# Two-layer vision tower, layer-1 attention: first pair's transposed features fetched in layer 0's feed-forward into an older tile; normed pairs in six buffers and made first in their step

## The chip, the cores and the metric

The kernel runs on one core of one Trainium2 chip. The metric is the device time of one execution in microseconds (us), as the median of three executions. All arithmetic is in fp32.

## The reference, cut to what matters

32 images of 256x256 pixels are cut into 256 patches each; a patch becomes a token of 256 features. Two layers follow, each with an attention part and a feed-forward part, and each part adds its result to `h`. The change lies where layer 0's feed-forward ends and layer 1's attention begins, so only these two are shown (biases, all of which the kernel keeps, are left out here).

```
# layer 0, feed-forward on x = layernorm(h): 127 tokens of each image are selected by a weight
y = gelu(sel @ w1) @ w2 * w_sel          # sel: the selected rows of x
h = h + (x with y added at the selected rows)

# layer 1, attention on x = layernorm(h)
key   = tanh(gelu(x @ Wk1) @ Wk2) * freq * pi
query = tanh(gelu(x @ Wq1) @ Wq2) * freq * pi
V     = x @ Wv
retrieved[l] = sum over m <= l of V[m] * sum_k cos(key[m,k] - query[l,k])
retrieved    = retrieved / sqrt(position * 64)
h = h + x + layernorm(retrieved) @ Wo
```

After it comes layer 1's feed-forward, a per-head attention with four expert queries, which takes the last third of the time.

## The kernel before

Everything is one function, `vit_tower`. `h` stays in SBUF for all 32 images (`H[b]`, 128 partitions x 2 halves x 256 features). The order of instructions on each engine is written out by hand (`tc.manual_schedule`, for all that follows here): each engine runs its instructions in program order, and a tile's buffers (`bufs=n`) make a new writer wait for the last readers of the buffer that it takes over.

**Layer 0's feed-forward** works on quads of four images. Its loop runs t from 0 to 31 (`END_C` is 32, line 907), and `step_c(t)` (line 901) issues by the table `ORDER_C` what of each quad is due: `hidden_c` (w1 and GELU), `made` (w2; each image's result `cy` is written to DRAM as `results` by SyncE, line 871), `fetch` (the results gathered back by rank with indirect DMAs on GpSimd, line 879), `update` (the result added into `H` and the row statistics taken, lines 890, 124, 125). The table reaches past the loop: the last quad's `fetch` and `update` come at 32, 33 and 34, which are issued within layer 1's attention (at its t = 6, 9 and 12).

**Layer 1's attention** works on 16 pairs of two images. What it needs per pair, with the lines that the prediction speaks of:

- `norm_d` (825): the normed tokens `x = h * rstd + (1 - mean * rstd)`, on VectorE. For each image two small operations on `d_one` (832, 833) and two on 128x256 (835). Pairs 0 and 1 are made inside layer 0's loop, at its t = 30, into buffers of `cx`; all later pairs into buffers of `dx`, of which there are four, so two pairs.
- `blocks_d` (841): VectorE turns the pair in blocks of 32x32 (197) into `dxB` (pairs 0 and 1: into `cs`), and SyncE writes it to the DRAM tile `c_turned` (200), which has two buffers.
- `moved_d` (934), by `moved` (202): SyncE reads `c_turned` back, rearranged to feature-major order, into `dxT` (203), which has two buffers. The two DMAs together with the blocks make the transpose.
- `hidden` (937): TensorE multiplies `dxT` with `wk1` (i = 0) and `wq1` (i = 1), eight matmuls each, and ScalarE applies GELU into `dg0`/`dg1` (946).
- `phases` (948): TensorE takes `dg` through `wk2`, `wq2`; ScalarE tanh into `dturn` (963); VectorE wraps the phase in `dz` (965 to 969); ScalarE takes the sine (970).
- `match` (972): TensorE multiplies the sines; VectorE masks into `dat` (985).
- `memory` (988): TensorE multiplies the normed tokens (`cx` or `dx`) with `dat`; ScalarE copies to `dm` (998). These are the last reads of the pair's normed tokens on TensorE.
- `output` (1001): TensorE multiplies `dm` with `wvo`; VectorE takes statistics (1009, 1010); GpSimd makes `d_rs` (149, 150).
- `add_output` (1016): VectorE adds the scaled result to `H` (1019), which also frees the four PSUM banks of `output`. `stats_e` (1021): the row statistics for the next part, with `rs_e` on GpSimd.
- `residual_d` (846): GpSimd adds the normed tokens and a constant row to `H`, four operations per pair (849, 850).

The loop of this stage (line 1030) runs over t, three steps to a pair; `do(step, which)` issues `which` for the pair u with t = 3u + step. For t above 5 the order is: steps with t = 1 mod 3: `add_output` of the pair two back, `match` of the pair before, `stats_e` two back, `residual_d`; steps with t = 2 mod 3: `hidden` of pair u, `memory` of pair u - 1, and then `norm_d`, `blocks_d`, `moved_d` of pair u + 1; steps with t = 0 mod 3: `phases` of u and `output` of u - 1. The first steps are special: at t = 1 `moved_d` of pair 0; at t = 2 `hidden` of pair 0 and `moved_d` of pair 1; at t = 5 `hidden` of pair 1 with `match` of pair 0 between its halves, `residual_d` of pair 1, and then the norm of pair 2.

Layer 0's pools are closed ahead of this loop (lines 925, 926), and the pools `d_2` and `d_8` take over their memory: `dxT`, `dg`, `dz` in `d_2`; `dat`, `dm`, `dx`, `dxB` in `d_8`. The pool `c_x`, with the eight `cx` buffers and the one tile `blocks` (4 KB per partition; its last use is the turning of layer 0's last quad), stays open to the end of the attention (line 1074).

Of the kernel before, what the change touches and what calls it, by code (L numbers as in the profile page):

```python
# [33 lines left out]
F32 = mybir.dt.float32  # L34
# [6 lines left out]
P = 128  # L41
B, N, D = 32, 256, 256
NC = N // P
# [37 lines left out]
def vit_tower(tc, a, out):  # L81
# [15 lines left out]
    def bank():  # L97
        return ppool.tile([P, 512], F32, name="bank", tag="bank")

    def col(name, i=0):  # L100
        c = COLS[name][0] + i
        return cols[:, c : c + 1]
# [12 lines left out]
    def mm(o, lhsT, rhs, first=True, last=True):  # L115
        nc.tensor.matmul(o, lhsT, rhs, start=first, stop=last)  # L116
# [4 lines left out]
    def stats(st, i, c, x):  # L121

        six = spool.tile([P, 6], F32, name="six")
        nc.vector.bn_stats(six, x)  # L124
        nc.vector.bn_aggr(st[:, i, c, :], six)
# [26 lines left out]
    def pow_rstd_of(pair, b, images):  # L152
        st, rs, i = at(pair, b)
        q = slice(i * NC, (i + images) * NC)
        pow_rstd(rs[:, q], st.rearrange("p i c s -> p (i c) s")[:, q, 1])

    def new_stats(name):
        return [
            (
                cpool.tile([P, HALF, NC, 2], F32, name=f"st_{name}{k}", tag=f"st{k}", bufs=2),  # L160
                cpool.tile([P, HALF * NC], F32, name=f"rs_{name}{k}", tag=f"rs{k}", bufs=2),
            )
            for k in range(2)
        ]

    def at(pair, b):

        st, rs = pair[b // HALF]
        return st, rs, b % HALF
# [22 lines left out]
    def blocks_turned(y, xs, d):  # L192

        y5 = y.rearrange("p (f s t) -> p s f t", f=4, t=32)
        n = 8 // len(xs)
        for j, x in enumerate(xs):
            nc.vector.transpose(
                y5[:, j * n : (j + 1) * n], x.rearrange("p c (k f t) -> p (c k) f t", k=2, f=4)
            )
        nc.sync.dma_start(d.rearrange("i q x -> (i q) x"), y)  # L200

    def moved(xT, d):
        nc.sync.dma_start(xT, d.rearrange("i q (f x) -> (q f) i x", f=4))
        return xT.rearrange("p i (s k t) -> p k s i t", k=2, t=32)
# [12 lines left out]
    px = passing_x.enter_context(tc.tile_pool(name="c_x", bufs=1, reuse_waits="tile"))  # L217
# [86 lines left out]
    with (  # L304
# [7 lines left out]
        for k, n in enumerate(PARTS):  # L312
            f = sum(PARTS[:k])
            x, w = pw.tile([P, n, N], F32, name=f"patch0_{k}"), pw.tile([P, n, D], F32, name=f"tokW{k}")
# [4 lines left out]
        p = bank()  # L319
# [116 lines left out]
    with (  # L436
# [80 lines left out]
        def ranks(b0, p):  # L517
            for j in range(2):
                rank_c(b0 + j, *normed_c[b0][j], p[:, j * N : (j + 1) * N])

        def norms_c(b0):
            normed_c[b0] = [norm_c(b0 + j) for j in range(2)]

        def residuals_c(b0):
            for j in range(2):
                residual_c(b0 + j, normed_c[b0][j][0])
# [126 lines left out]
    for i in range(2):  # L653
        s, t = slice(i * HD, (i + 1) * HD), slice((1 - i) * HD, (2 - i) * HD)
# [186 lines left out]
    def blocks_d(b0, s, pool, name, shape, bufs):  # L841
        y = pool.tile(shape, F32, name=name, bufs=bufs)
        s.d = pdram.tile([4, 32, 4 * N], F32, name="c_turned", bufs=2)
        blocks_turned(y.rearrange("p j d -> p (j d)"), s.xs, s.d)
# [7 lines left out]
    with region_c:  # L852
        st_d = new_stats("d")

        def hidden_c(b0, s, half):
            if half == 0:
                s.hT = p2.tile([P, 8, 4 * P], F32, name="hT")
            for m in range(4 * half, 4 * half + 4):
                p = bank()
                for k in range(2):  # L860
                    mm(p, w1[:, k, m * P : (m + 1) * P], s.f[:, k], k == 0, k == 1)
                nc.scalar.activation(s.hT[:, m, :], p, AF.Gelu_apprx_tanh, bias=col("b1", m))  # L862

        def made(b0, s, half):
            for j in range(2 * half, 2 * half + 2):
                p = bank()
                for m in range(8):
                    mm(p[:, 0:D], s.hT[:, m, j * P : (j + 1) * P], w2[:, m, :], m == 0, m == 7)
                y = p2.tile([P, D], F32, name="cy", bufs=4)
                nc.vector.tensor_tensor(y, p[:, 0:D], row_c("b2"), ALU.add)  # L870
                nc.sync.dma_start(results[b0 + j][:], y)

        def fetch(b0, s, half):
            s.y = s.y if half else []
            for b in range(b0 + 2 * half, b0 + 2 * half + 2):
                y = px.tile([P, NC, D], F32, name="cx", bufs=8)
                for c in range(NC):
                    k = b * NC + c
                    nc.gpsimd.indirect_dma_start(
                        y[:, c, :], None, results[b][:], bass.IndirectOffsetOnAxis(rank_of[:, k : k + 1], 0)  # L880
                    )
                s.y.append(y)

        def update(b0, s, half):
            for j in range(2 * half, 2 * half + 2):
                b = b0 + j
                st, rs, i = at(st_d, b)
                for c in range(NC):
                    k = b * NC + c
                    nc.vector.scalar_tensor_tensor(  # L890
                        H[b][:, c, :], s.y[j][:, c, :], w_kept[:, k : k + 1], H[b][:, c, :], ALU.mult, ALU.add
                    )
                    stats(st, i, c, H[b][:, c, :])
            pow_rstd_of(st_d, b0 + 2 * half, 2)

        ORDER_C = ((0, hidden_c, 0), (1, hidden_c, 1), (2, made, 0), (-3, blocks_c, 0), (-2, moved_c, 0), (-8, first_ranks, 0),
                   (3, made, 1), (4, fetch, 0), (5, fetch, 1), (5, update, 0), (6, update, 1))

        def step_c(t):
            for at_step, do, j in ORDER_C:
                u, r = divmod(t - at_step, 4)
                if r == 0 and 0 <= u < B // 4 and (u > 1 or do is not first_ranks):
                    do(4 * u, quads[u], j)

        END_C = 4 * (B // 4 - 1) + 4
        pairs = [Pair() for _ in range(B // 2)]
        preparing = prepare()
        for t in range(END_C):  # L910
            if t == 0:
                norms_c(B - 2)
                residuals_c(B - 2)
            if t == END_C - 2:
                for u in range(2):
                    norm_d(2 * u, pairs[u], px, "cx", 8)
                for u in range(2):
                    blocks_d(2 * u, pairs[u], p0, "cs", [P, 4, D], 2)
            step_c(t)
            if t < 2:  # L920
                ranks(B - 4 + 2 * t, turn_weights(B - 4 + 2 * t))
            if t >= 8:
                next(preparing, None)
        passing.close()
# [5 lines left out]
    with (  # L930
# [99 lines left out]
        for t in range(3 * (NP - 1) + 8):  # L1030
            def do(step, which, *more):
                u, r = divmod(t - step, 3)
                if r == 0 and 0 <= u < NP:
                    which(2 * u, pairs[u], *more)

            last = t == 3 * NP + 1
            if t == 1:
                do(1, moved_d)
            if not last:
                do(7, add_output)  # L1040
            if t != 4:
                do(4, match)
            if last:
                output(B - 4, pairs[NP - 2], (3,))
                add_output(B - 4, pairs[NP - 2])
            do(7, stats_e)
            if t != 4:
                do(1, residual_d)
            do(2, hidden, 0)
            if t == 2:  # L1050
                do(2, hidden, 1)
                moved_d(2, pairs[1])
            elif t == 5:
                do(2, hidden, 1, (0,))
                match(0, pairs[0])
                do(2, hidden, 1, (1,))
            else:
                do(2, hidden, 1)
            do(5, memory)
            do(3, phases)  # L1060
            if t == 5:
                residual_d(2, pairs[1])
            if t > 4:
                do(-1, norm_d, p8, "dx", 4)
                do(-1, blocks_d, p8, "dxB", [P, 2 * NC, D], 1)
                do(-1, moved_d)
            if t == 3 * NP:
                output(B - 4, pairs[NP - 2], (0, 1, 2))
            else:
                do(6, output)  # L1070
            if t in (6, 9, 12):
                step_c(END_C + (t - 6) // 3)
# [5 lines left out]
    with (  # L1078
# [452 lines left out]
        p = bank()  # L1531
# [385 lines left out]
```

## Time and profile before

| what | value |
|---|---|
| median of three runs | 1897.08 us (1895.45 to 1898.73) |
| the profiled execution: its own time, its span | 1897.49 us, 1895.8 us |
| TensorE busy over the span | 1845.8 us, 97% |
| VectorE, ScalarE, GpSimd busy | 1350.6, 792.0, 758.1 us |
| mean granted TensorE clock | 0.985 of full speed |
| layer 0's last matmul of `made` ends | at 912.3 us |
| first matmul of layer 1's attention | at 917.26 us |
| the attention's last pair begins | at 1218.02 us |
| layer 1's feed-forward begins on TensorE | at 1247.7 us |

The page gives busy times by engine, a chain of work followed back from the last instruction, and groups of instructions with the idle time of the engine just ahead of them and what ended it. The timeline lists instructions of an engine with start and duration in us, merged where alike follow each other ("x8"), with the idle time before them in brackets. "PE" is TensorE, "PEld" its weight loads, "DVE" VectorE, "ACT" ScalarE, "POOL" GpSimd, and "SPq" SyncE's queue of DMA issues. A table by windows gives each engine's busy time in each stretch and the granted clock (PEclk).

### The profile page before, as it was taken

To read this page: it belongs to the slowest core of one execution; us is meant where nothing else is said; L and a number is where in the kernel's file an instruction comes from. 1 tells how busy PE (TensorE), PEld (TensorE's weight loads), DVE (VectorE), ACT (ScalarE), POOL (GpSimd) and SP (SyncE) were. 2 spreads that over 40 slices of the span, in tenths; PEclk is the share of its full clock that TensorE was granted. 3 is DMA by queue.
4 is the path that set the end of the run, shared out by engine and by line. 5 is a ranking of instruction groups with operands and counts; after the bars stand their busy time and mean duration, and the time that the engine had idled before them with its cause. 6 is when DMAs were issued, how large, how long until landed. Compare 5 with 4: busy or idle time off the path is not lost.

```text
span 1895.8 us, 36643 instructions
## 1 busy us (share of the span) xinstructions
PE 1845.8 (97%) x14548; PEld 1305.8 (69%) x14548; DVE 1350.6 (71%) x3287; ACT 792.0 (42%) x1608; POOL 758.1 (40%) x792
## 2 busy tenths in 40 slices
PE   9999999999999999999899999999999999999993
PEld 8887566666666676766555555578787878788872
DVE  2335477878786574535387777645999999999988
ACT  0001222222222212122334444457888787878772
POOL 1224133434343344334253333324455554545453
PEclk9999999999999999999999999999999999999995
DMA  9440221212121143333221111101222222222212
GB/s 312 152 150 20 42 62 42 72 40 64 37 65 36 64 136 117 108 100 100 71 67 45 49 63 45 45 18 30 52 64 52 64 55 64 54 64 52 63 41 58
DMA packets 148354, 134.33 MB, mean 71 GB/s; under 512 B 68560, under 2 KB 123344, under 8 KB 147792
## 3 DMA queue, kind: packets, MB, share of 16 engines
q1 hardware_dynamic: 141456, 114.34, 21.4%
q0 software_dynamic: 6144, 16.79, 2.9%
q8 instruction: 117, 1.92, 0.4%
q10 hardware_dynamic: 576, 0.79, 0.1%
q14 instruction: 61, 0.50, 0.1%
HBM read 66.34 MB, written 40.89 MB: 57 GB/s over the span
## 4 chain that ended last, share of the span: by engine, by line
PE 92%; DVE 4%; DMA 2%; issue 1%; ACT 0%; SPq 0%; POOL 0%; DVEq 0%
PE bank L116 90%; PE bank L808 2%; DMA dxT<-c_turned 2%; PE bank L514 0%; DMA patch<-in_patches_dram 0%; DVE fout L1411 0%; DVE fout L1425 0%; DVE dx L835 0%; DVE eo L1289 0%; DVE six L124 0%; DMA b_turned<-blocks 0%; DMA bxT<-b_turned 0%; DVE ranges L1312 0%; DVE fout L1414 0%; DVE ey L1374 0%
## 5 line engine op out<-in xcount | busy, mean ns | idle before, releaser
L1208 POOL TENSOR_SCALAR_AFFINE_SELECT et<-et 128x512 f32<-128x512 f32 (+1 forms) x192 | 165.8, 876 | 203.1 <-ACT et L1199 201.1
L1199 ACT ACTIVATE et<-bank 128x512 f32<-128x512 f32 x384 | 207.7, 630 | 30.6 <-PE bank L116 30.3
L116 PE MATMUL bank<-ev,et 128*64 128x68 f32 (+1 forms) x6144 | 200.6, 226 | 0.0
L116 PEld LDWEIGHTS bank<-ev,et 128*64 128x64 f32 x6144 | 193.0, 138 | 5.7 <-issue 4.7
L116 PE MATMUL bank<-g,sx 64*128 64x512 f32 (+1 forms) x512 | 177.6, 486 | 0.0
L116 PE MATMUL bank<-g,sw 64*128 64x512 f32 (+1 forms) x512 | 177.2, 486 | 0.0
L116 PE MATMUL bank<-tokW,patch 128*128 128x256 f32 x768 | 167.9, 382 | 0.6 <-DMA patch<-in_patches_dram 0.6
L116 PEld LDWEIGHTS bank<-tokW,patch 128*128 128x128 f32 x768 | 147.2, 192 | 21.6 <-DMA tokW<-in_tokW_dram 1.4
L116 PE MATMUL bank<-bxT,w_wuv 128*128 128x512 f32 x300 | 132.9, 598 | 2.7 <-DMA bxT<-b_turned 2.7
L1228 ACT COPY eo<-bank 128x280 f32<-128x280 f32 x256 | 96.1, 395 | 70.0 <-PE bank L116 63.3
L862 ACT ACTIVATE hT<-bank,cols 128x512 f32<-128x512 f32 x64 | 44.0, 687 | 186.7 <-PE bank L116 186.7
L116 PEld LDWEIGHTS bank<-g,sx 64*128 64x128 f32 x512 | 93.2, 187 | 31.7 <-issue 22.9
L116 PE MATMUL bank<-wvo,dm 128*128 128x512 f32 x256 | 114.3, 599 | 0.0
L116 PE MATMUL bank<-w_wo,gT 128*128 128x256 f32 x512 | 113.2, 380 | 0.0
L116 PE MATMUL bank<-attn,bv 128*128 128x256 f32 x512 | 113.1, 379 | 0.0
L116 PE MATMUL bank<-w_w,hT 128*128 128x256 f32 x512 | 112.3, 380 | 0.0
L116 PE MATMUL bank<-xsel,w_w 128*128 128x512 f32 x256 | 111.4, 593 | 0.0
L116 PEld LDWEIGHTS bank<-attn,bv 128*128 128x128 f32 x512 | 97.4, 190 | 19.4 <-issue 7.2
L124 DVE BATCH_NORM_STATS2 six<-h 128x6 f32<-128x256 f32 x256 | 105.5, 412 | 4.4
L116 PEld LDWEIGHTS bank<-w_w,hT 128*128 128x128 f32 x512 | 97.1, 190 | 15.4 <-issue 2.9
L116 PEld LDWEIGHTS bank<-g,sw 64*128 64x128 f32 x512 | 93.3, 187 | 20.0 <-issue 9.9
L116 PEld LDWEIGHTS bank<-w_wo,gT 128*128 128x128 f32 x512 | 97.4, 190 | 13.2 <-DVE gT L487 0.2
(273 smaller groups left out, 3751.3 us busy)
## 6 DMA issues: line engine op xcount, KB each, us to landing
patch<-in_patches_dram SPq DMA_DIRECT2D x31, 768.0 KB, 4.7
dxT<-c_turned SPq DMA_DIRECT2D x16, 512.0 KB, 3.8
sw<-sx SPq DMA_DIRECT2D x64, 128.0 KB, 2.3
out_dram<-fout SPq DMA_DIRECT2D x32, 256.0 KB, 2.4
both<-fxT SPq DMA_DIRECT2D x62, 128.0 KB, 2.3
both<-hx SPq DMA_DIRECT2D x62, 128.0 KB, 2.3
b_turned<-blocks SPq DMA_DIRECT2D x56, 128.0 KB, 3.3
bxT<-b_turned SPq DMA_DIRECT2D x56, 128.0 KB, 3.1
```

The source lines that it names most:

```text
L116: nc.tensor.matmul(o, lhsT, rhs, start=first, stop=last)
L124: nc.vector.bn_stats(six, x)
L808: nc.tensor.transpose(p[:, o : o + P], x[:, c, k * P : (k + 1) * P], ident)
L862: nc.scalar.activation(s.hT[:, m, :], p, AF.Gelu_apprx_tanh, bias=col("b1", m))
L1199: nc.scalar.activation(t2[:, i, :], p, AF.Exp)
L1208: nc.gpsimd.affine_select(out=own, in_=own, pattern=[[0, 2 * n_e], [1, P]], compare_op=ALU.is_ge, fill=0.0, base=0, channel_multiplier=-1,)
L1228: nc.scalar.copy(im.o[:, g * OC : (g + 1) * OC], p[:, 0:OC])
```

## The change

Three edits, all in program order or in buffers; no arithmetic is changed.

1. The read of pair 0's transposed features from `c_turned` is issued in layer 0's loop at t = 30, right after `blocks_d` of pairs 0 and 1, and lands in the tile `blocks` of the pool `c_x` instead of a buffer of `dxT`. The `moved_d` at t = 1 of the attention loop goes.
2. `dx` has six buffers instead of four, so three pairs.
3. From t = 5 on, `norm_d`, `blocks_d` and `moved_d` of pair u + 1 are issued ahead of `hidden` of pair u, not after `memory` of pair u - 1 and `phases`.

```diff
                 for u in range(2):
                     blocks_d(2 * u, pairs[u], p0, "cs", [P, 4, D], 2)
+                pairs[0].f = moved(
+                    px.tile([P, 4 * N], F32, name="blocks", bufs=1).rearrange("p (i x) -> p i x", i=4), pairs[0].d
+                )
             step_c(t)
...
             last = t == 3 * NP + 1
-            if t == 1:
-                do(1, moved_d)
             if not last:
                 do(7, add_output)
...
             if t != 4:
                 do(1, residual_d)
+            if t > 4:
+                do(-1, norm_d, p8, "dx", 6)
+                do(-1, blocks_d, p8, "dxB", [P, 2 * NC, D], 1)
+                do(-1, moved_d)
             do(2, hidden, 0)
...
             if t == 5:
                 residual_d(2, pairs[1])
-            if t > 4:
-                do(-1, norm_d, p8, "dx", 4)
-                do(-1, blocks_d, p8, "dxB", [P, 2 * NC, D], 1)
-                do(-1, moved_d)
             if t == 3 * NP:
```

As the built programs show, the order on ScalarE, GpSimd and TensorE is the same before and after. On VectorE only pair 2's norm and blocks change places: they come ahead of the first pair's two `dat` operations instead of after them. On SyncE the read of pair 0's features moves from behind the last four `results` writes to ahead of them. The waits of `norm_d` on TensorE are gone. The tiles of `d_2` and `d_8` lie at other addresses than before, since the pools hold other numbers of buffers.

## The prediction

> **What bounds the kernel now.** I read the page's chain first, then the chain in order of time for the stage that is edited, then what TensorE and VectorE wait for there.
>
> ```profile
> PE 92%; DVE 4%; DMA 2%; issue 1%; ACT 0%; SPq 0%; POOL 0%; DVEq 0%
> PE bank L116 90%; PE bank L808 2%; DMA dxT<-c_turned 2%; PE bank L514 0%; DMA patch<-in_patches_dram 0%; DVE fout L1411 0%; DVE fout L1425 0%; DVE dx L835 0%; DVE eo L1289 0%; DVE six L124 0%; DMA b_turned<-blocks 0%; DMA bxT<-b_turned 0%; DVE ranges L1312 0%; DVE fout L1414 0%; DVE ey L1374 0%
> ```
>
> TensorE holds 92% of the chain; the only transfer of weight on it is `dxT<-c_turned`, the one that the change moves. In order of time:
>
> ```profile
> 912.78 0.32 SPq L871
> ...
> 913.21 4.01 DMA dxT<-c_turned
> ...
> 917.26 51.74 PE bank L116 x192
> ...
> 1050.56 3.86 DMA dxT<-c_turned
> ...
> 1054.55 36.88 PE bank L116 x140
> ```
>
> At 912.78 SyncE issues layer 0's last `results` write, behind it the read of pair 0's features, and TensorE starts when that lands. From 1050 on the chain enters through `dxT` every second pair, 40.9 us apart. TensorE's timeline gives the sizes:
>
> ```profile
> 917.26 5.95 PE L116 MATMUL bank<-dxT,w_wk 128*128 128x512 f32 x8 [4.96 <-DMA dxT<-c_turned]
> 923.05 3.60 PE L116 MATMUL bank<-dxT,w_wq 128*128 128x512 f32 x8
> ...
> 1033.81 3.70 PE L116 MATMUL bank<-dxT,w_wk 128*128 128x512 f32 x8
> ...
> 1054.55 3.67 PE L116 MATMUL bank<-dxT,w_wk 128*128 128x512 f32 x8 [0.54 <-DMA dxT<-c_turned]
> ```
>
> The pair at 1033.81 starts with no idle time before it, 20.10 us after the pair at 1013.71. That is the floor of a pair: TensorE was never idle in it. The next takes 20.74. Why `dxT` comes late is in VectorE's waits and timeline:
>
> ```profile
> DVE dx L835 <- PE bank L116: 33.3, 12, 3.8
> PE bank L116 <- DMA dxT<-c_turned: 9.5, 8, 5.0
> ```
>
> ```profile
> 955.95 0.73 DVE L835 TENSOR_SCALAR dx<-h,rs_d,d_one 128x256 f32<-128x256 f32 x2
> ...
> 1022.16 2.59 DVE L835 TENSOR_SCALAR dx<-h,rs_d,d_one 128x256 f32<-128x256 f32 x2 [3.85 <-PE bank L116]
> ```
>
> From pair 4 on the norm waits for TensorE's `memory` of two pairs earlier (12 times, 33.3 us), since four `dx` buffers hold two pairs. Pair 3 at 955.95 took buffers that nobody had used and didn't wait.
>
> [...] granted clock 0.50 from 917 to 921 us after an idle time of 4.96, 1.00 from 923 on; the waits of 0.5 to 1.2 us lower it nowhere. [...] two `dx` operations take 0.73 us alone and 2.59 beside GpSimd's additions of 1.26 each. [...] a `c_turned` write takes 2.6 us and a `dxT` read 3.8, one behind the other.
>
> **Part 1, the first pair's read.** The write of pair 0's blocks is issued at 898.91 and lands after 2.8, at 901.7; the read behind it takes 3.8 and lands at about 905.5. TensorE asks at 912.3: 6.8 us to spare. What it gives: the idle 4.96, and the slow clock. With it the eight `wk1` matmuls took 923.05 - 917.26 = 5.79 us start to start, against 1037.35 - 1033.81 = 3.54 at full clock: 2.25 more. Together **7.21 us**. ScalarE is idle then (17.89 us before its first GELU), its table loaded from 901.90; its first `dg1` write waits for the reads of `cs` that it now overlays, which land by about 903.
>
> What it moves: on SyncE's queue the read is now ahead of layer 0's last four `results` writes. SyncE stands from 900.4 (second blocks write issued) to 901.7, issues by 902.1, and the first result comes at 902.42, so nothing slips. If it did, only the gathers on GpSimd wait for `results`, and the last quad's start at 951.10, with 36 us of cover. Pair 1's read stays last, issued at 913.2, landing at 917.1. TensorE asks for it at 912.3 + (928.45 - 917.26) - 2.25 = 921.2: 4.1 us of cover. The tile `blocks` was last read by a DMA at step 25 of layer 0, long done.
>
> **Part 2, pair 2 at t = 5.** On VectorE its norm and blocks (936.35 to 939.73, 3.38 us, GpSimd idle) now stand ahead of `dat`, which waited 3.04 us at that place for TensorE's `match`. `dat` is 0.34 later: its first half at 936.3, where TensorE's `memory` starts at 937.13. Cost 0; without that cover 0.34.
>
> **Part 3, the steady pairs.** On all engines the order is as before; the wait on TensorE goes. The norm starts when `d_one` is done: 1018.31, which is 4.60 us after the pair's first matmul at 1013.71, instead of 8.45. How long norm and blocks take beside GpSimd's `rs_e` and `residual_d` isn't shown for just this place, so I bound it: 3.38 with GpSimd idle (pair 2); 4.34 for pair 3, which ran as the changed pairs will (955.59 to 959.93); 4.92 as now (1022.16 to 1027.08); 5.86 at worst (979.41 to 985.27). I take 5.0. Then 4.60 + 5.0 + 2.65 (write) + 3.85 (read) + 0.14 = 16.2 us after the pair's first matmul, against 20.10 when the next pair asks. Cover 3.9, and 3.0 at the worst bound, so every `dxT` wait from pair 4 on goes.
>
> What is late next: the sines, which arrive 0.7 us ahead of `match` in the late pairs and come earlier too, as VectorE gets to them when `dturn` is there (1026.25, not 1027.00); PSUM banks, where `hidden`'s third block needs the first `add_output` of the pair before, done 1.1 us after the pair's start and needed at 3.54. Only at t = 9 and 12 four updates of layer 0 stand before `add_output`; at 974.39 TensorE waits for it, 974.39 - 970.42 - 3.54 = 0.43 late. I keep that twice, since after the change TensorE sets the pace at both. [...]
>
> The sum: pairs 2 to 15 start 267.73 us apart now (950.29 to 1218.02, 13 periods). After: 13 x 20.10 + 2 x 0.43 = 262.16. Gain **5.57 us**. The rest, from 1218.02 on, is not touched: the same instructions behind the same TensorE (581.3 us busy of 582 until 1800), and the tiles of the new layout wait only for work long done.
>
> Together 7.21 + 5.57 = 12.78. Against the profiled execution's own 1897.49 (span 1895.8 and 1.7 around it): 1884.7. The median lies 0.41 below that execution, so **1884.3**.
>
> **The rivals.**
> - *Only the first gap closes* (8%): another loop, as VectorE to sine to `match`, holds the pairs at their present pace. For it: in five late pairs a weight load stands 0.8 us for the sine. Against: TensorE's matmuls run on there, and those sines were late because the norm was. 1897.1 - 7.2 = 1889.9.
> - *The first edit doesn't do what it says* (5%): the wait moves to pair 1's read, or the one SyncE queue delays it. Against: 4.1 us of cover. 1897.1 - 5.6 = 1891.5.
> - *The clock drops anyhow* at the change of stage (7%): the gap goes but the 2.25 stay, 1886.6. Against: it dropped nowhere behind shorter waits.
> - *Slower* (2%): the norms now run wholly beside GpSimd[...]. It decides from where norm and blocks pass 20.10 - 4.60 - 6.64 = 8.9 us, and the kernel is slower than before from about 8.9 + 0.5 + 7.2/13 = 9.9 on. At 11 (eight small operations, each held for one of GpSimd's 1.26) a period is 22.2 us, 13 x (22.2 - 20.6) = 21 lost, 7.2 gained: 1911. Against: GpSimd has four additions per pair, 5.2 us, and the worst seen is 5.86.
> - The forecast has the rest, 78%.
>
> **How the numbers follow.** The forecast's own spread is about 1881.5 to 1887: the three runs of before lie within 1.7 us of their median, the 0.86 at t = 9 and 12 may go, half the short waits may stay (2 us). The third rival lies inside. Below 1881 and above 1888 I leave the first, second and fourth rivals, 15%, and a few per cent of tail. A measurement can tell about 0.2%, 3.8 us, from no change: faster is below 1893.3, which the forecast and the first and third rivals give, 93%, and some of the second, 2%; its noise gives 3% for the same; slower 2%.
>
> **What would show it.** Right: the first `wk1` matmul of the attention follows the last of `made` with under 1 us between, its eight take 3.5 to 3.7 us, PEclk is 1.00 there; no wait of `dx` for TensorE; pairs 20.1 us apart, twice 20.5; single `dx` operations of over 1 us. Wrong: a `dxT` wait at the second pair (Part 1), periods still alternating (Part 3), a norm of over 8.9 us, or new idle time behind 1205 us.

## The result, and the profile after

| | before | after |
|---|---|---|
| median, first comparison (4 runs each) | 1896.45 us | 1885.59 us (1883.73 to 1888.36) |
| ratio of the two, 95% interval | | 0.9942 (0.9924 to 0.996) |
| the profiled execution: own time, span | 1897.49, 1895.8 us | 1888.36, 1886.7 us |
| mean granted TensorE clock | 0.985 | 0.987 |
| from the first matmul of layer 0's last `made` to the first `wk1` matmul of pair 15 ("the stretch") | 319.70 us | 307.22 us |

The change saves 10.9 us in this comparison and 9.1 us in the profiled execution; 12.8 were forecast for both. The stretch in which the change works became 12.48 us shorter. So the first question after "does the mechanism hold?" is where 1.6 us went.

The page of the kernel after has the chain's shares by engine; `dxT` (2% before) is no longer among what the chain goes through, and the 1% of transfers that is left is the load of the patches:

```profile
PE 94%; DVE 3%; DMA 1%; issue 1%; ACT 0%; SPq 0%; POOL 0%; DVEq 0%
PE bank L116 92%; PE bank L808 2%; DMA patch<-in_patches_dram 1%; PE bank L514 0%; DVE six L124 0%; DVE fout L1412 0%; DVE fout L1426 0%; DVE eo L1290 0%; DMA bxT<-b_turned 0%; DMA b_turned<-blocks 0%; DVE ranges L1313 0%; DVE fout L1415 0%; DVE h L890 0%; DVE ey L1375 0%; DVE er L1325 0%
```

The same chain in order of time (start, us, what), from 869 on. Where before it went through `dxT` at 913 and then at pairs 4 and 5 and every second pair, it now stays on TensorE from layer 0 to the attention's last pair and leaves it only twice on the way, for VectorE, from 964 to 970 and from 985 to 990:

```profile
869.89 94.44 PE bank L116 x361
...
969.74 15.24 PE bank L116 x56
...
989.86 0.38 DVE h L1022
...
990.37 238.40 PE bank L116 x952
```

TensorE's timeline of the kernel after:

```profile
901.14 13.98 PE L116 MATMUL bank<-w_w,hT 128*128 128x256 f32 x64
914.95 3.60 PE L116 MATMUL bank<-blocks,w_wk 128*128 128x512 f32 x8
918.39 3.60 PE L116 MATMUL bank<-blocks,w_wq 128*128 128x512 f32 x8
...
969.74 3.67 PE L116 MATMUL bank<-dxT,w_wq 128*128 128x512 f32 x8 [0.28 <-DVE h L1022]
...
1027.17 3.70 PE L116 MATMUL bank<-dxT,w_wk 128*128 128x512 f32 x8
...
1047.30 3.70 PE L116 MATMUL bank<-dxT,w_wk 128*128 128x512 f32 x8
```

No idle time stands ahead of 914.95, and eight `wk1` matmuls take 3.44 us start to start (918.39 - 914.95) instead of 5.79. Pairs follow each other at 20.13 us (1047.30 - 1027.17) without a wait. The one kind of idle time left is in brackets at 969.74: VectorE's `add_output`, line 1022 in this kernel. The table by windows (length; busy us and instructions of PE, PEld, DVE, ACT, POOL; granted clock; DMA share; GB/s) shows the clock across the change of stage at 1.00 throughout:

```profile
901.00:914.90 13.90, 13.90 (x65) 12.13 (x64) 7.01 (x19) 1.97 (x2) 1.84 (x3) 1.00 0.41 142
914.90:918.40 3.50, 3.50 (x11) 1.56 (x10) 0.42 (x1) 0.69 (x1) 3.34 (x4) 1.00 0.40 109
```

### The profile page after: what moved, and what is told of

Read it like the earlier page. It is cut to its first block, busy times and chain, and to the rows that moved or that the text cites. A ratio compares the mean times of both kernels' runs of the same rounds, so it can differ in the third digit from the quotient of the medians.

```text
span 1886.7 us, 36621 instructions
## 1 busy us (share of the span) xinstructions
PE 1843.9 (98%) x14548; PEld 1303.2 (69%) x14548; DVE 1348.2 (71%) x3287; ACT 792.4 (42%) x1608; POOL 759.8 (40%) x792
## 4 chain that ended last, share of the span: by engine, by line
PE 94%; DVE 3%; DMA 1%; issue 1%; ACT 0%; SPq 0%; POOL 0%; DVEq 0%
PE bank L116 92%; PE bank L808 2%; DMA patch<-in_patches_dram 1%; PE bank L514 0%; DVE six L124 0%; DVE fout L1412 0%; DVE fout L1426 0%; DVE eo L1290 0%; DMA bxT<-b_turned 0%; DMA b_turned<-blocks 0%; DVE ranges L1313 0%; DVE fout L1415 0%; DVE h L890 0%; DVE ey L1375 0%; DVE er L1325 0%
```

## The experiments

Each run is read in the same stretch of its trace: from the first matmul of the last `made` to the first `wk1` matmul of pair 0 ("gap"; before 18.94 us), on to pair 2 ("start"; before 33.03), and from pair 2 to pair 15 ("13 periods"; before 267.73). My theory: these are three separate losses, one idle gap, one slow clock after it, and late `dxT` reads in the steady pairs; they add up, and nothing outside the stretch moves. The rivals are those of the prediction, and after the result one more: the change costs 1.5 us somewhere outside the stretch.

| run | median us, runs | ratio, 95% interval | gap | start | 13 periods | stretch |
|---|---|---|---|---|---|---|
| before (profile) | see text | 1 | 18.94 | 33.03 | 267.73 | 319.70 |
| after (profile) | 1885.59, 4 | 0.9942 (0.9924 to 0.996) | 13.81 | 30.68 | 262.73 | 307.22 |
| e1_after | 1884.12, 5 | 0.9929 (0.9916 to 0.9943) | 13.81 | 30.68 | 262.72 | 307.21 |
| e1b_after | 1886.24, 5 | 0.9941 (0.9927 to 0.9954) | 13.82 | 30.67 | 262.73 | 307.22 |
| e2_read_only | 1887.78, 5 | 0.995 (0.9937 to 0.9964) | 13.82 | 30.67 | 267.61 | 312.10 |
| e3_six_only | 1892.83, 8 | 0.9973 (0.9962 to 0.9983) | 18.88 | 33.68 | 262.72 | 315.28 |
| e4_six_and_order | 1892.37, 7 | 0.997 (0.9959 to 0.9981) | 18.93 | 33.09 | 262.73 | 314.75 |
| e9_read_last | 1891.97, 11 | 0.9977 (0.9968 to 0.9986) | 18.90 | 33.56 | 262.71 | 315.17 |
| e5_warm_gap | 1897.81, 12 | 1.0003 (0.9994 to 1.0012) | 22.45 | 30.67 | 267.53 | 320.65 |
| e5b_warm_half | 1895.69, 20 | 0.9991 (0.9985 to 0.9998) | 18.78 | 30.75 | 267.67 | 317.20 |
| e6_write_twice | 1885.03, 2 | 0.9939 (0.9919 to 0.9959) | 13.82 | 30.67 | 263.61 | 308.10 |
| e7_write_thrice | 1902.9, 4 | 1.003 (1.0015 to 1.0046) | 13.82 | 30.67 | 284.06 | 328.55 |
| e8_update_by_image | 1883.18, 5 | 0.9933 (0.992 to 0.9947) | 13.82 | 30.67 | 261.71 | 306.20 |

The kernel before, run beside them: 1897.47 (beside e1 to e4), 1897.16 (beside e5, e6, e7, e9) and 1896.86 (beside e1b, e5b, e8).

**The changed kernel again** (no edit), twice:

> The changed kernel once more, timed in five rounds. My sum: from the first matmul of layer 0's last made step to the first matmul of pair 15, 12.5 us less than before in any execution (the first profile showed 319.70 against 307.22). Whole time: 12 to 13 us below before if the start of the kernel is like before's; 10 to 11 if a later start, as in the first profile (2.8 us later at that step), belongs to the changed kernel. Rival: the late start is chance, and then this stretch begins at 898 to 901 us with either kernel.

> The changed kernel once more, beside the same runs of the kernel before as the two others, for the size of its gain: my theory (12.5 us in the stretch from the last made to pair 15, and nothing elsewhere) says 1884.5, within 1 us, against 1897; the first result, 1885.6 against 1896.5, would be due to starts of the kernel that vary by 1 to 3 us. Rival: the part of the kernel outside the stretch loses 1.5 us through the change; then the gain stays at 11 us in the median.

The stretch is the same to 0.01 us in all three profiles, but the medians are 1885.59, 1884.12 and 1886.24. What differs lies ahead of the stretch and behind it. The last `made` begins at 901.14 in the first profile, at 897.38 and 901.43 in the two others, and at 898.32 in that of before. The change can't be the cause, since its first instruction, the early read, is issued only at 904.55. Two things vary there: the wait for the patches (0.6 us before, 2.6 after, 1.2 in e1_after), and TensorE's clock. The record of the granted clock has single intervals of 3.41 us at half clock: ahead of the stretch one at 198.20 us in the profile before and one at 201.64 in that after. What such an interval costs shows in the chains: the piece of 208 TensorE instructions that starts near 200 us takes 61.93 us in before, and 60.49 in e1 and e8. The piece of 736 ahead of it takes 159.11 in before, 159.10 in e1 and 159.11 in e8, but 160.68 in e5b and 160.79 in e1b, as if with such an interval in it (an estimate). The stretch begins between 897.3 and 897.8 in e1, e2, e7 and e8, and between 899.4 and 899.6 in e3, e4, e5, e5b, e6 and e9.

Behind the stretch it is alike. From layer 1's feed-forward (its first `w_hl` matmul) to the end, ten profiles take 646.7 to 647.3 us, and three (e2, e4, e6) 645.4 to 645.9. The profiles before and after, two of the ten, have an interval at half clock there, at 1816.12 and 1805.91 us. So a median of four or five runs carries 1 to 2 us of this. Pooled, 14 runs of the changed kernel have a median of 1884.3 and a mean of 1885.3, 69 of the kernel before 1897.1 and 1897.0: a gain of 12.8 by medians, 11.7 by means with a standard error of about 0.5. The means alone would still allow the rival of a loss of 1.5 us outside the stretch. The profiles don't: from pair 15 to the end the changed kernel takes 678.3, 677.8 and 677.9 us, the kernel before 677.8, and what stands ahead of the stretch runs before the change begins.

**The first edit alone**: the kernel before with the early read.

```diff
                     blocks_d(2 * u, pairs[u], p0, "cs", [P, 4, D], 2)
+                pairs[0].f = moved(
+                    px.tile([P, 4 * N], F32, name="blocks", bufs=1).rearrange("p (i x) -> p i x", i=4), pairs[0].d
+                )
...
-            if t == 1:
-                do(1, moved_d)
```

> Only edit 1: pair 0's read issued in layer 0 into the older tile; four dx buffers, norm in its old place. Theory (the two parts add up, and nothing follows late behind the first): 4.96 idle + 2.3 slow clock = 7.3 us less, 1889 to 1890; no wait for dxT before pair 2; clock 1.00 throughout; pairs from 4 on 20.6 us apart on the mean as before. Rival (starting earlier only moves the wait to pair 1's read, or VectorE's updates eat it): under 4 us less, with a dxT wait at pair 1 or longer waits at pairs 3 to 5.

The stretch is 7.60 us shorter. The median is 9.7 us lower, more than expected; its profile is one of the three that are shorter behind the stretch (645.5 us). Gap and start are those of the full change; the periods still alternate as before, and the waits list of this run keeps the late read, as a total in us, its times and the longest:

```profile
PE bank L116 <- DMA dxT<-c_turned: 4.4, 7, 1.1
```

**The other two edits, together and one alone**: e4 is the changed kernel with the read of pair 0 back at t = 1; e3 is the kernel before with only six buffers.

```diff
-                do(-1, norm_d, p8, "dx", 4)
+                do(-1, norm_d, p8, "dx", 6)
```

> Only six dx buffers; order and read as before. Theory (the buffer wait is the whole of the steady part, and the order edit matters for no pair but the second): 5.0 to 5.3 us less, 1891 to 1892; no wait of dx for TensorE; pairs 20.13 apart, twice 20.6. Rival (the order edit is needed for it): pairs still alternate 20.1 and 20.7, under 2 us less.

> Six dx buffers and the new order, but pair 0's read in its old place. Theory: as six buffers alone, 5.0 to 5.3 us less, the gap of 5 us at the attention's first matmul and its slow clock still there; against six buffers alone within 0.5 us. Rival (the order brings gain of its own, or stretches pair 0's dat): over 1 us off six buffers alone.

Both have 262.7 us for the 13 periods, as after. So the buffers alone carry the gain of the steady pairs, and the waits of `dx` for TensorE (33.3 us before, 33.1 in e2) are gone from the lists of both runs, as from that of the changed kernel. That the norm is issued first in its step adds nothing, as it is the same order on VectorE for every pair but pair 2. The parts add: 7.60 (e2) + 4.95 (e4) = 12.55, against 12.48 for all. The waits lists of e3 and e4 keep the first gap, here e3's:

```profile
PE bank L116 <- DMA dxT<-c_turned: 4.9, 1, 4.9
```

e3's start is 0.65 longer than that of before, which no theory had. The windows (columns as above) of the kernel before, then of e3, start where TensorE fell idle, and are cut where the recorded clock changes:

```profile
912.30:915.00 2.70, 0.00 (x0) 0.00 (x0) 0.42 (x1) 0.00 (x0) 2.62 (x3) 1.00 0.35 70
915.00:921.82 6.82, 4.56 (x6) 1.98 (x7) 0.00 (x0) 0.69 (x1) 6.46 (x6) 0.50 0.42 145
921.82:925.00 3.18, 3.18 (x9) 1.46 (x8) 0.00 (x0) 0.72 (x2) 0.00 (x0) 1.00 0.00 0
```

```profile
913.43:917.37 3.94, 0.00 (x0) 0.00 (x0) 0.42 (x1) 0.00 (x0) 3.78 (x4) 1.00 0.57 141
917.37:924.19 6.82, 5.86 (x7) 2.52 (x8) 0.00 (x0) 0.69 (x1) 5.30 (x5) 0.50 0.26 91
924.19:927.00 2.81, 2.81 (x8) 1.23 (x7) 0.00 (x0) 1.00 (x2) 0.00 (x0) 1.00 0.00 0
```

The half clock lasts 6.82 us in both, but it begins 2.70 us after TensorE fell idle in the one and 3.94 in the other. So 4.56 us of it fall on work before and 5.86 in e3. Half of that is lost, 2.28 and 2.93, which is the 0.65. Behind the same read the eight `wk1` matmuls take 5.79 (before), 5.85 (e4), 6.32 (e9) and 6.43 us (e3), and the first edit is worth 7.5 us against the profiled execution of before, and about 8.1 against one whose clock falls as in e3 (an estimate: 5.13 + 33.68 - 30.68).

**Tile or queue?** The first edit does two things: another tile, and another place in SyncE's queue. e9 keeps the tile, and issues the read after layer 0's loop, behind the last four `results` writes.

> The changed kernel, with pair 0's read into the tile blocks issued at the end of layer 0's loop, behind the last four results writes, as before the change. Theory (the place on SyncE's queue made the read late, not the tile that it lands in): the gap of 5 us and its slow clock are back, 18.9 us from the last made step to the first wk1 matmul and 314.5 to 314.8 to pair 15. Rival (dxT's buffer, freed late, held the read): 13.8 us, 307.2.

SyncE's queue in e9 and the wait that it causes on TensorE:

```profile
903.55 10.68 SPq L871 DMA_DIRECT2D results<-cy  x4
914.32 0.39 SPq L203 DMA_DIRECT2D blocks<-c_turned  x1
```

```profile
918.35 6.48 PE L116 MATMUL bank<-blocks,w_wk 128*128 128x512 f32 x8 [4.93 <-DMA blocks<-c_turned]
```

The gap is back in full, and the stretch of 315.17 lies 0.4 over the expectation, as its eight `wk1` matmuls took 6.32 us, not 5.79. It is the place in the queue that made the read late: its data had been in DRAM since about 903 (the write of pair 0's blocks was issued at 900.31, and took 2.8 us in the kernel before), and the read stood behind writes which wait for TensorE's last matmuls. The tile `blocks` only makes the early place possible.

**Wait or clock?** To part the two losses of the gap, TensorE multiplies zeros while the read is under way, in the kernel before (t = 1; the products are not used). e5 has 20 such calls, e5b 10.

```diff
             if t == 1:
                 do(1, moved_d)
+                for i in range(8):
+                    p = bank()
+                    for _ in range(2 + i % 2):       # e5b: range(1 + (i < 2))
+                        mm(p[:, 0:N], zero[:, 0:P], zero)
```

> The kernel before, with 20 matmuls of zeros (128x256, 4.4 us, in eight banks that nobody reads) on TensorE ahead of the attention's first matmul, in its idle time of 5 us; the rest of the computation is unchanged. Theory (the idle time drops the clock, and the slow clock costs 2.3 us of the first edit's gain): first wk1 to first wq1 matmul 3.44 us instead of 5.79; from the last made step to pair 15 317.3 us, 2.3 to 2.4 less than before; the attention still begins 18.9 us after that step. Rival (the stage's first matmuls are slow for another reason, as their weights or the banks): still 5.8 us, 319.7.

> The kernel before, with 10 multiplications of zeros (20 matmul instructions of 128x256, about 4.4 us) in the idle time ahead of the attention's first pair: half as many as in the run e5_warm_gap, where they ended 3.5 us after the first pair's features had landed. They compute nothing that is used. My theory says that the lost time in that gap has two parts, the wait for the read (4.96 us) and the slow clock after it (2.25 to 2.4 us), and that the second goes if TensorE is kept busy through the first. Then made to wk1 stays at 18.9 us, wk0 to wk2 falls from 33.03 to 30.67, the stretch is 317.3 us instead of 319.7, and the time is 2.4 us (0.13%) below that of the kernel before. Rival: the clock drops at this change of stage whatever runs; then wk0 to wk2 stays near 33.0 and the time is the same.

e5 missed its total: each call is two matmul instructions (x40 in the trace), so the zeros took 8.80 us and ended 3.5 us after the read had landed. It still answers the question, as the start is 30.67 us and the clock is 1.00 there (from 917 to 926 us). e5b, of the right length, gives both numbers:

```profile
913.34 4.48 PE L116 MATMUL bank<-zero 128*128 128x256 f32 x20
918.31 3.67 PE L116 MATMUL bank<-dxT,w_wk 128*128 128x512 f32 x8 [0.49 <-DMA dxT<-c_turned]
921.81 3.60 PE L116 MATMUL bank<-dxT,w_wq 128*128 128x512 f32 x8
```

The gap stays (18.78), the eight `wk1` matmuls take 3.50 at a clock of 1.00, and the stretch falls by 2.50. The median is 1.2 us lower, with an interval of 0.4 to 2.8 that holds the 2.4 expected. So idle time is what lowers the clock here, not the change of stage, and 2.3 to 2.4 us of the 7.5 that were lost in the profiled execution of before were the clock.

**How much cover do the steady pairs have?** The chain norm, blocks, write, read is made longer by writing each pair's blocks to `c_turned` again (the same bytes), once more in e6 (from pair 6 on) and twice more in e7, in the changed kernel.

```diff
+            for _ in range(1 if b0 >= 12 else 0):    # e7: 2
+                nc.sync.dma_start(s.d.rearrange("i q x -> (i q) x"), y.rearrange("p j d -> p (j d)"))
```

> The changed kernel, with the write of blocks to DRAM done twice, one after the other, for pairs 6 to 15 (2.65 us more before the read of dxT). Theory (a read lands 2.8 to 3.8 us before TensorE asks): 0 to 0.3 us more from the last made step to pair 15, 307.2 to 307.5, no dxT wait over 0.2 us. Rival (there is no such cover; the read is just in time as before the change): 1.3 us or more for every second pair, over 6 us in all.

> The same write done three times (5.3 us more). Theory: the cover of 2.8 to 3.8 us is used up; a pair waits 1.5 to 2.5 us for dxT, and since the norm of a pair follows the wvo matmuls of one period earlier, the loop closes over two periods: waits at every second pair, 41.7 to 42.7 us for two, 7 to 12 us more in the stretch (314 to 320). Rival (loop over one period): every pair 1.5 to 2.5 us longer, 15 to 25 us more.

One more write (2.6 us) costs nothing in all periods but one, of 21.05 us, where TensorE waits 0.85 us for `dxT`. With that the stretch is 308.10, above the 307.5 expected. In that pair SyncE's queue shows the first write taking 5.0 us (1176.08 to 1181.09, where the next pair's takes 2.6):

```profile
1176.08 0.32 SPq L200 DMA_DIRECT2D c_turned<-dxB  x1
1181.09 0.32 SPq L846 DMA_DIRECT2D c_turned<-dxB  x1
1183.73 0.37 SPq L203 DMA_DIRECT2D dxT<-c_turned  x1
1196.20 0.32 SPq L200 DMA_DIRECT2D c_turned<-dxB  x1
1198.80 0.32 SPq L846 DMA_DIRECT2D c_turned<-dxB  x1
```

Two more (5.2 us) bring the waits back, and with them more than their own length. TensorE's timeline of e7:

```profile
1027.14 5.37 PE L116 MATMUL bank<-dxT,w_wk 128*128 128x512 f32 x8 [3.30 <-DMA dxT<-c_turned]
...
1071.33 5.37 PE L116 MATMUL bank<-dxT,w_wk 128*128 128x512 f32 x8 [2.19 <-DMA dxT<-c_turned]
...
1115.55 3.67 PE L116 MATMUL bank<-dxT,w_wk 128*128 128x512 f32 x8 [2.21 <-DMA dxT<-c_turned]
```

So the cover lies between 2.6 and 5.2 us. e7's 13 periods are 21.3 us longer than after, where 7 to 12 were expected. The waits come at every second pair only up to pair 10, and then at pairs 11 to 14 too: seven waits, 14.7 us in sum. Behind three of them the matmuls are slow as well: eight take 5.37 us instead of 3.70 at 1027.14 and 1071.33, where the granted clock falls to 0.50, and 6.65 at 1203.22.

Behind the wait of 2.19 us the clock was 0.50, behind one of 2.21 it stayed at 1.00. In e7 the recorded clock changes at 1028.31, 1031.72, 1072.68 and 1076.10 us, so 1, 12 and 1 times 3.41 us apart. Windows of this length, counted on from these changes, two around each of the two waits:

```profile
1069.27:1072.68 3.41, 1.35 (x3) 0.68 (x4) 2.92 (x7) 0.00 (x0) 0.43 (x1) 1.00 0.36 125
1072.68:1076.10 3.42, 3.42 (x5) 1.35 (x4) 3.17 (x14) 0.69 (x1) 1.47 (x3) 0.50 0.00 0
...
1113.64:1117.05 3.41, 1.50 (x4) 0.82 (x5) 3.09 (x9) 0.00 (x0) 0.25 (x1) 1.00 0.35 123
1117.05:1120.46 3.41, 3.41 (x10) 1.50 (x9) 3.17 (x14) 1.37 (x2) 1.64 (x3) 1.00 0.00 0
```

TensorE worked 1.35 us of the first interval, so it was idle for 2.06, and the next interval ran at half clock, though TensorE was at work again by then. Of the other interval it was idle for 1.91 us, and the clock stayed. The traces of before and after, counted on in the same way from their own changes, agree: seven intervals at full clock were followed by half clock, with TensorE idle for 2.07 to 2.93 us of each, and in none of the others was it idle for more than 1.55. That the idle time within one such interval is what parts the two waits is my estimate from these three traces; no run varied it alone.

**The last two long periods.** Pairs 3 and 4 still take 20.65 and 20.63 us. In the changed kernel layer 0's last four images are updated two at t = 9 and two at t = 12 (not four at once, as the expectation has it). e8 takes them apart, one image at a time at t = 11, 14, 17 and 20, so that they no longer stand as a block ahead of `add_output` on VectorE. `update_one` is `update` for one image.

```diff
-            if t in (6, 9, 12):
-                step_c(END_C + (t - 6) // 3)
+            if t in (6, 9):
+                fetch(B - 4, quads[-1], t // 3 - 2)
+            if t in (11, 14, 17, 20):
+                update_one(B - 4, quads[-1], (t - 11) // 3)
```

> The changed kernel, with layer 0's last four updates (four DVE updates of h with their statistics, for the last quad) taken apart: one image each at t = 11, 14, 17 and 20 of the attention loop instead of four images at once at t = 12; the gathers stay at t = 6 and 9. My theory says that the two periods that are left above 20.13 us (20.65 and 20.63 in the changed kernel, at pairs 3 and 4) are TensorE waiting for add_output behind these updates on VectorE. Then no period stays above 20.3, and the stretch from the last made to pair 15 is 306.2 us instead of 307.2. Rival: the two periods are long for another reason (the norm of a pair beside GpSimd, or the gathers on GpSimd); then both stay at 20.6 and the stretch at 307.2. A second rival: the updates only spread, and each of the four steps loses a quarter, so the stretch stays at 307.2 with four periods of 20.4. The median moves by 1 us or less, which five rounds can hardly tell; the stretch decides.

```profile
962.02 3.70 PE L116 MATMUL bank<-dxT,w_wk 128*128 128x512 f32 x8
965.56 3.60 PE L116 MATMUL bank<-dxT,w_wq 128*128 128x512 f32 x8
...
982.15 3.70 PE L116 MATMUL bank<-dxT,w_wk 128*128 128x512 f32 x8
```

The idle time that stood ahead of the `wq1` matmuls is gone, all 13 periods are 20.13, and the stretch is 306.20, as expected. This version is the quickest measured, 1883.18 us; its lead over the changed kernel is 1.02 us in the trace, less than the medians can tell apart.

## Why the prediction was right

**Part 1, the first pair's read: right, 0.3 too small.** Forecast 7.21; the gap gave 5.13 (18.94 - 13.81) and the slow clock 2.35 (33.03 - 30.68), together 7.48. e5b shows the second without the first. The bracket's 4.96 is counted from the last matmul's recorded end; without a wait the next matmul starts 0.17 before that end (901.14 + 13.98 - 914.95), and the gap closes by that too; the clock term was worked out against 3.54 us for eight matmuls, where 3.44 is what they take at this place. The forecast took the clock's price as fixed; e3 and e9 show that it lies between 2.3 and 3.0 us, so that it came out so near owes something to chance. The early read is issued at 904.55; with the 3.85 us that these reads took before it lands at 908.4 (an estimate), 6.5 us ahead of the first matmul, where 6.8 were forecast. Pair 1's read caused no wait, as forecast. e9 shows what the cover is worth: behind the `results` writes it is gone.

**Part 2, pair 2 at t = 5: right, no cost.** Start to pair 2 is 30.68 us in the changed kernel and 30.67 in e2, which has the old order there.

**Part 3, the steady pairs: mechanism right, 0.57 too much.** Forecast 262.16 us, measured 262.73. Two terms were mis-sized. The floor was read as 20.10 from a pair which followed a wait; a pair that follows another unhindered one takes 20.13, so 13 x 0.03 = 0.39. The two delays by layer 0's updates were put at 0.43 each and are 0.52 and 0.50, so 0.16. e8 shows that these updates were the cause.

**The cover.** I had the norm start 4.60 us after the pair's first matmul; it starts 5.30 after it, since 4.60 was read in a pair that TensorE had begun late. VectorE, GpSimd and SyncE in a steady pair after, which began at 1027.17:

```profile
1033.91 2.77 DVE L835 TENSOR_SCALAR dx<-h,rs_d,d_one 128x256 f32<-128x256 f32 x2
1036.60 1.29 DVE L197 STREAM_TRANSPOSE dxB<-dx 128x512 f32<-128x512 f32 x2
```

```profile
1033.92 1.27 POOL L849 TENSOR_TENSOR h<-h,dx 128x512 f32<-128x512 f32 x1
1035.26 1.26 POOL L850 TENSOR_TENSOR h<-h,add_row 128x512 f32<-128x512 f32 x1
```

```profile
1037.92 0.32 SPq L200 DMA_DIRECT2D c_turned<-dxB  x1
1040.55 0.37 SPq L203 DMA_DIRECT2D dxT<-c_turned  x1
```

The norm and blocks end at 1037.89, 5.4 us after they began at 1032.47. The read is issued at 1040.55; nobody waits for it, so that the trace doesn't show when it lands. With the 3.85 us that it took before it is there at 1044.4 (an estimate), and TensorE asks at 1047.30: 2.9 us of cover, 4.0 in a pair whose norm was held less (1.69 instead of 2.77). The forecast had 3.9, and 3.0 at its worst bound. As the trace shows, two `dx` operations lie against two GpSimd additions and end within 0.2 us of them; the two before, at 1032.84 beside GpSimd's `rs_e`, take 0.76. In the kernel before, an operation on `d_one` that takes 0.13 at 1017.98 took 1.23 us at 980.07, and ended within 0.1 us of the addition beside it. Why they end together no run here shows. The longest norm with blocks in the changed kernel is 5.4 us, where the slower rival needed 8.9, so that rival had no room. e7 shows by other means what that rival would have done: once the chain is 5.2 us longer, the periods grow, by 21.3 us in 13.

**The sum.** 12.78 forecast, 12.48 in the stretch, 10.9 in the first comparison, 12.8 by the medians of all runs and 11.7 by their means. The sum is off by no more than 0.30 because Part 1 was 0.27 too small and Part 3 0.57 too large, and that the pooled medians give the forecast's own number is chance. The missing 1.6 us of the first comparison lie in how long the first 900 us and the last 650 take in single executions, not in a step of the prediction. The rivals *only the first gap closes* and *the first edit doesn't do what it says* fall with e4 and e2, and *the clock drops anyhow* with e5b. What the prediction held against that rival, that the clock dropped behind no shorter wait, is so in this stage (1.00 from 921.83 to 1218), but not in the whole trace of before: it was 0.50 from 198.20 and from 1816.12, behind waits of 2.66 and 2.07 us.

## What to carry to other kernels

A transfer whose data have long been ready can be late only because of what stands ahead of it in its issuing queue (behind the `results` writes the read was issued at 914.32 us in e9, and TensorE waited 4.93 for it; ahead of them at 904.55, with no wait); move its place, and find a tile that is already free, so that the place is allowed. When a producer waits for a consumer two rounds back, buffers for one more round can remove the whole wait, as here, and a new order of issue is worth nothing, as long as it stays the same on the producer's engine. What the wait was worth is read on the engine that sets the pace: 33.3 us of VectorE's waits were 5.0 us of TensorE's time. And take the floor of a loop from two unhindered rounds in a row, since a round behind a wait flatters it.

## What was not expected of the hardware

- An idle time of TensorE of 2.19 us was followed by the half clock (e7 at 1071.33), one of 2.21 us wasn't (at 1115.55). Of the 3.41 us ahead of 1072.68 TensorE was idle for 2.06, of those ahead of 1117.05 for 1.91.
- The half clock came in whole intervals of 3.41 us behind the waits for `dxT`, one (e7 from 1072.68) or two (before from 915.00, e3 from 917.37), and it could begin after TensorE had resumed work (e7 at 1072.68, 1.35 us after). After the same wait of 4.9 to 5.0 us it cost 2.3 (before) to 3.0 us (e3), by how much of it fell on work.
- A 512 KB write to DRAM, which takes 2.6 us in nearly every pair, once took 5.0 (e6 at 1176.08).
